# A norm's mean from added channel chunks and one matmul, with new plan costs and ring sizes

## The chip, the cores and the metric

The kernel runs on one core of a Trainium2 chip. The core has five engines that matter here: TensorE (matrix products, called PE in the profile), VectorE (DVE), ScalarE (ACT), GpSimd (POOL) and SyncE (SP), which issues nearly all DMAs. The metric is the device time of one execution in microseconds (us); lower is better. The time before is 3247.18 us, the median of three runs (3243.28 to 3256.7).

## What is computed

The input `x` has 8 images of 384 channels and 1024 pixels, in fp32. Everything below is per pixel (token) unless it says otherwise. The reference, cut to what matters:

```python
def _ln_c(v, eps=1e-6):                       # the norm over channels
    m = jnp.mean(v, axis=1, keepdims=True)
    s = jnp.var(v, axis=1, keepdims=True)
    return (v - m) / jnp.sqrt(s + eps)
...
# conv part: a selective state-space layer and an MLP
t = (t - mu) * rsqrt(var + 1e-05) * ln_w + ln_b
xm, z = split(t @ in_proj_w.T)                # 384 -> 2 x 768
xc = silu(causal_conv3(xm) + conv_b)
dt, Bm, Cm = split(xc @ x_proj_w.T)           # 24, 16, 16
dt = softplus(dt @ dt_proj_w.T + dt_proj_b)
h = exp(dt * A) * h + dt * xc * Bm            # scan over the 1024 tokens, 768 x 16 states
y = (sum_n(h * Cm) + xc * D) * silu(z)
t = gelu(y @ out_proj_w.T @ mlp_w1.T + b) @ mlp_w2.T + b
x = x + t
# ffn part: only images 0 to 4 get one, images 5 to 7 leave it out (zero rows of the quantiser)
t = x;  t = t + quant(gelu(quant(norm(t) @ sign(W1).T + b1)) @ sign(W2).T + b2)
```

Each image is a group of its own for the absolute maximum by which `quant` scales.

## The kernel before

Channels lie on the 128 partitions, in `KC` = 3 chunks of 128; the 1024 tokens are worked in two halves of `T` = 512. For image (batch) b there are four pieces of work:

- `s1` (L648): the norm, the input projection (`p_in`, `p_z`), the convolution, `p_dbc`, `p_dt`, and the products `dtx` = `xc` times `dt`. Results go to DRAM tensors.
- `s2`/`scan` (L812, L825): the scan, in 12 steps `m` per batch. A step loads `dtx_r` and two `dt_r` tiles, each broadcast over partitions by the DMA; for each of four quads of states POOL multiplies by B (L941, `product`), ACT takes two exponentials into PSUM tiles `da` (L550), DVE runs two scans (L966), POOL or DVE multiplies by C, and TensorE sums into `py` (L906). Batches 0 and 7 run by halves with a carried state, the other six over all 1024 tokens.
- `s3` (L1000): output projection (`p_out`) and MLP (`p_h`, `p_o`).
- `ffn` (L1204): norm, two binarised products (`p_y`), two quantisations; batches 0 to 4.

Nothing of the order is written by hand. Every piece of work is an `Op` with an engine and a cost in us, and `Plan.run` (L246) walks through time on these costs, picks the next op of an engine by rank, and emits the instructions in that order. An op can name another engine in `others`, and goes there as a guest when that engine could start it at least `HOST` = 0.3 us before its own engine is free, and be done before the work of its own. Ranks: the scan first, then `s1` up to the next batch (at first up to batch 4), then `s3` and `ffn`; DVE and POOL take ready work that isn't scan work first (L281 to L284). When TensorE would stand idle longer than 0.7 us, filler matmuls (`spare`, L444) are put in. On the chip each engine then runs its list in order and waits on semaphores.

Tiles come from rings: a ring of n buffers lets n tiles of that name live at once. Those that the change touches: `front` (7; pairs of `xc`, `z` and `dt` in s1), `w_f` (3; s1's weights), `dt_r` (3; two used in each scan step), `sq` (1; the square in a norm, the `dtx` tiles before their store, the diagonal in `quant_scale`). `mm` (3) is the PSUM ring of matmul outputs.

The norm (L583) runs 26 times: 16 in s1, 10 in ffn. Its mean before: `columns` (L586) sums over channels with 12 column-tiled matmuls of 32 output rows each, four abreast, so the sums of 512 tokens lie as four strips of 128; ACT (or DVE) scales them by -1/C; `spread` (L601) brings them to all partitions with four matmuls against slices of the identity, and DVE adds the result to the three chunks (L622). The variance then goes the same way by `Square`, `columns`, a turn, a power on POOL, and `spread` with `turned=True`.

Plan costs that the change touches: `MM` (a 128x512 fp32 matmul), `SWITCH` (added per `py` batch), `LAG` (how much before its end an engine counts as free), `c_pair` (POOL's product), and the landing time of a DMA in `Plan.add` (L205).

Of the kernel before, what the change touches and what calls it, by code (L numbers as in the profile page):

```python
# [27 lines left out]
AF = mybir.ActivationFunctionType  # L28
# [42 lines left out]

MM = 0.86
SWITCH = 0.22
# [13 lines left out]
LOAD_TABLE = 1.29  # L87
LAG = {"ACT": 0.09, "DVE": 0.08}

# [9 lines left out]
def c_pair(n):  # L99
    return 0.22 + n * 0.00188  # L100

# [78 lines left out]
class Op:  # L180
    __slots__ = (
        "engine", "cost", "emit", "prio", "slack", "table", "size",
        "wants", "next", "ready", "tiles", "others", "settle", "land",
    )


class Plan:
# [12 lines left out]
    def add(self, engine, cost, emit, r=(), w=(), claim=(), table=None, size=0, others=None,  # L200
            land=1.6, rate=350e3):
        op = Op()
        op.engine, op.cost, op.emit, op.table = engine, cost, emit, table
        op.others, op.settle = others or {}, None
        op.size, op.land, op.prio = 0.03 + size / rate, land + 0.2, (*self.prio, len(self.ops))  # L205
        op.next, op.ready, op.tiles = [], 0.0, []
        op.slack = SLACK if self.prio[0] < 0 else 0.0
# [38 lines left out]
    def run(self):  # L246
# [5 lines left out]
        free["PE"] = 2 * SIGNAL  # L252
        table, dma_free, clock = None, 0.0, Clock()
        left, scanned = len(self.ops), 0
# [17 lines left out]
        def choose(e, now, able):  # L272
            able = [op for s, op in able if s <= now]
            if e == "ACT":
                same = [op for op in able if op.table == table and table != "exp"]
                plain = [op for op in able if op.table in (None, "exp")]
                able = same if table is not None and same else plain or able
                if len(self.spare.ring.free) <= SCARCE:
                    able = [op for op in able if self.spare.ring in map(ring_of, op.tiles) and (
                        op.table in (None, "exp", table))] or able  # L280
            if e in ("DVE", "POOL"):  # L281

                able = [op for op in able if op.prio[0] > 0 and op.ready <= now - PATIENCE] or [
                    op for op in able if op.prio[0] == 0] or able  # L284
            return min(able, key=rank)
# [27 lines left out]
        while left:  # L313
# [28 lines left out]
            if e == "PE":  # L342
                while now - free[e] > IDLE and self.spare.ring.free[0:] and (
                    self.spare.ring.free[0] + SIGNAL <= free[e]
                ):

                    ring = self.spare.ring
                    heapq.heappop(ring.free)
                    self.spare.real = ring.make(self.spare.shape, self.spare.name)
                    self.fill()  # L350
                    free[e] = clock.run(free[e], MM / 2)
                    heapq.heappush(ring.free, free[e])
            for t in taken_by(op):
                heapq.heappop(t.ring.free)
                t.ring.taken[t.lane] += 1
                t.real = t.ring.make(t.shape, t.name)
            op.emit()
            cost = op.cost
            if op.table is not None and op.table != table:
                cost += LOAD_TABLE  # L360
                table = op.table
            end = clock.run(now, cost) if e == "PE" else now + cost
            free[e] = end - LAG.get(e, 0.0)
            if e == "SP":
# [19 lines left out]
class Layer:  # L384
    def __init__(self, ctx, tc, a, out):
# [9 lines left out]
        def ring(tag, bufs, where=sbuf):  # L395
# [6 lines left out]

            "front": ring("front", 7), "t_f": ring("t_f", 2), "w_f": ring("w_f", 3),
            "dbc": ring("dbc", 1), "halo": ring("halo", 2),

            "dt_r": ring("dt_r", 3), "dtx_r": ring("dtx_r", 2), "u": ring("u", 3),
            "xr": ring("xr", 1), "zr": ring("zr", 1), "state": ring("state", 1),
# [137 lines left out]

    def act(self, out, in_, func, cost, r, w, table=None, **kw):

# [4 lines left out]
            }),  # L552
            r=r, w=w, table=table,
        )

    def affine(self, out, in_, r, w, bias=0.0, scale=1.0, n=T, pool=False):
# [21 lines left out]
        else:  # L578
            others = {"DVE": (c_dve(n) + (0 if isinstance(scale, float) else 0.15), on(nc.vector))}
        extra = 0.0 if plain else 0.09 if isinstance(scale, float) else 0.18  # L580
        self.plan.add("ACT", 0.16 + n * 0.00083 + extra, on_act, r=r, w=w, others=others)

    def norm(self, t, eps, scale):  # L583

        nc, add = self.nc, self.plan.add
        def columns(src, name):  # L586
# [35 lines left out]
        add("DVE", c_dve(KC * T), lambda: nc.vector.tensor_add(  # L622
            t.real, t.real, p_mean.real.unsqueeze(1).to_broadcast([P, KC, T])
        ), r=[p_mean], w=[t])
# [6 lines left out]
        p_turned = self.piece("mm", [P, G], "p_turned")  # L631
        add("PE", 0.3, lambda: nc.tensor.matmul(
            p_turned.real, var.real, self.ident[:, ::DQ], start=True, stop=True
        ), r=[var], w=[p_turned])
        rstd = self.piece("root", [P, G], "rstd")
        add("DVE", 0.1, lambda: nc.vector.tensor_scalar_add(rstd.real, p_turned.real, eps),
            r=[p_turned], w=[rstd])
# [10 lines left out]
    def s1(self, b):  # L648
# [45 lines left out]
        for half, cols in enumerate(HALVES):  # L694
# [58 lines left out]

            add("PE", 0.15 + KC * MM, low, r=[w, *all_m], w=[p_dbc], claim=[dbc])
            self.affine(lambda dbc=dbc: dbc.real, lambda p_dbc=p_dbc: p_dbc.real, [p_dbc], [dbc])
# [12 lines left out]
            for k in range(0, KD, 2):  # L768
# [14 lines left out]

                add("PE", MM + 0.2, two, r=[dbc, *dict.fromkeys(ws)], w=pds, claim=[dt.pieces[k // PER]])
                for i in range(2):
# [39 lines left out]
    def scan(self, b, half, state):  # L825
# [21 lines left out]
        for m in range(KC * per_p):  # L847
# [12 lines left out]
            def unit(name, p=p):  # L860
# [7 lines left out]
            xr = unit("xc")  # L868
            self.act(lambda py=py: py.real, lambda xr=xr: xr.real, AF.Identity, c_act(T),
                     r=[xr], w=[py], scale=skip[:, m : m + 1])  # L870
# [18 lines left out]
            for q in range(NQUAD):  # L889
# [43 lines left out]
    def scan_pair(self, u, cols, n, dts, dtxs, bq, cq, state, half, on_pool):  # L933
# [153 lines left out]
    def binarise(self, name, kt, n_out):  # L1087
# [25 lines left out]
        for ks, ms in pieces:  # L1113
# [11 lines left out]

            add("PE", 0.25 + MM, total, r=[w], w=[pm])
            if ks.stop == kt:
# [10 lines left out]
        p_mean = self.piece("mm", [P, NUM_GROUPS, 2], "p_means")  # L1138
        add("PE", 0.3, lambda: nc.tensor.matmul(
            p_mean.real, self.ones[:rows, :], sums.real[:rows], start=True, stop=True  # L1140
# [29 lines left out]
    def quant_scale(self, mx, n):  # L1170
# [11 lines left out]

        add("PE", 0.25, lambda: nc.tensor.matmul(
            p_max.real, self.ones, diag.real, start=True, stop=True
# [196 lines left out]
```

## Time and profile before

| what | value |
|---|---|
| median of 3 runs | 3247.18 us (3243.28 to 3256.7) |
| the profiled execution | 3251.59 us, span 3249.5 us |
| mean granted TensorE clock | 0.982 |
| PE busy | 3136.0 us |
| DVE busy | 2607.3 us |
| ACT busy | 2025.7 us |
| POOL busy | 2749.4 us |
| DMA | 751.89 MB, mean 231 GB/s |

The page lists busy time of each engine, the span in 40 slices of 81 us (a digit is tenths of busy time), the chain of work that ended last, groups of instructions by line, and the DMA issues. A group's row reads: line, engine, operation, output<-inputs, shapes, count | busy us, mean ns of one | idle before it and what ended that. A wait's row reads: who waited <- for whom: us in total, times, the longest. Matmul records are pipelined and an fp32 matmul shows as two records.

### The profile page before, as it was taken

What the parts mean: (1) busy time and instruction counts of PE and PEld (TensorE: products, weight loads), DVE (VectorE), ACT (ScalarE), POOL (GpSimd) and SP (SyncE); (2) the same over time, 40 slices, a digit from 0 to 9 for tenths busy, and PEclk for the clock granted to TensorE, in tenths of its full rate; (3) what the DMA queues carried; (4) which work ended last, traced back from release to release, by engine and by line L of the source; (5) the groups of instructions that cost most, each with busy time, mean ns of one, the idle gap of its engine ahead of it and who ended that gap; (6) DMA issues with size and microseconds to landing.
All of it is one profiled execution on the core that took longest, in us unless ns stands there. A gap on an engine that the chain in (4) does not pass through costs nothing.

```text
span 3249.5 us, 34179 instructions
## 1 busy us (share of the span) xinstructions
PE 3136.0 (97%) x11088; PEld 1308.8 (40%) x11088; DVE 2607.3 (80%) x2078; ACT 2025.7 (62%) x2406; POOL 2749.4 (85%) x1051
## 2 busy tenths in 40 slices
PE   9889899999999998999999999899999999999999
PEld 4333333334443344443443443343344454333334
DVE  3687788988979878887799798698798988787870
ACT  4777677785585656557655755466656465555651
POOL 1777888988889998998988999889999999889870
PEclk9899999999999999999999999999999999999999
DMA  6799778785785667858767666786776666656542
GB/s 214 257 319 302 230 247 284 273 282 192 251 308 190 200 208 268 284 199 273 233 238 283 209 202 209 271 276 223 247 253 235 220 210 212 220 175 195 158 126 79
DMA packets 348977, 751.89 MB, mean 231 GB/s; under 512 B 36480, under 2 KB 113792, under 8 KB 339584
## 3 DMA queue, kind: packets, MB, share of 16 engines
q1 hardware_dynamic: 348368, 749.61, 69.1%
q8 instruction: 89, 1.46, 0.2%
q14 instruction: 88, 0.72, 0.1%
q10 hardware_dynamic: 432, 0.09, 0.0%
HBM read 569.21 MB, written 180.36 MB: 231 GB/s over the span
## 4 chain that ended last, share of the span: by engine, by line
PE 69%; DVE 9%; ACT 7%; DMA 6%; POOL 5%; issue 3%; SPq 1%; DVEq 0%; POOLq 0%; ACTq 0%
PE p_y L534 18%; PE p_h L534 11%; PE p_o L534 11%; PE py L906 8%; PE p_z L534 6%; PE p_out L534 5%; PE p_in L534 5%; POOL u L941 4%; DVE u L966 4%; DVE da L966 2%; ACT da L550 2%; ACT L550 2%; PE p_dt L779 1%; PE spare L444 1%; DMA w_f<-in_in_proj_w 1%
## 5 line engine op out<-in xcount | busy, mean ns | idle before, releaser
L941 POOL TENSOR_TENSOR u<-dtx_r,bc 128x2048 f32<-128x2048 f32 (+1 forms) x360 | 1186.1, 3310 | 133.5 <-PE py L906 82.1
L550 ACT ACTIVATE da<-dt_r,a_neg 128x1024 f32<-128x1024 f32 (+1 forms) x960 | 898.9, 945 | 540.3 <-DVE u L966 306.8
L941 POOL TENSOR_TENSOR u<-u,bc 128x2048 f32<-128x2048 f32 (+1 forms) x274 | 901.2, 3292 | 148.0 <-DVE u L966 133.2
L966 DVE TENSOR_TENSOR_SCAN u<-da,u 128x1024 f32<-128x1024 f32 (+1 forms) x436 | 870.1, 2007 | 153.1 <-ACT da L550 75.3
L534 PE MATMUL p_h<-t,w_b 128*128 128x512 f32 x1152 | 515.5, 599 | 11.1 <-DMA w_b<-in_mlp_w 5.7
L534 PE MATMUL p_o<-g,w 128*128 128x512 f32 x1152 | 514.0, 600 | 9.9 <-DMA w<-in_mlp_w 5.3
L966 DVE TENSOR_TENSOR_SCAN da<-da,dtx_r 128x1024 f32<-128x1024 f32 (+1 forms) x192 | 382.7, 2016 | 91.1 <-POOL dtx_r L941 67.4
L941 POOL TENSOR_TENSOR dtx_r<-dtx_r,bc 128x2048 f32<-128x2048 f32 (+1 forms) x120 | 397.0, 3314 | 2.0
L534 PEld LDWEIGHTS p_o<-g,w 128*128 128x128 f32 x1152 | 215.7, 191 | 301.3 <-issue 273.4
L534 PEld LDWEIGHTS p_h<-t,w_b 128*128 128x128 f32 x1152 | 214.2, 190 | 298.9 <-issue 255.5
L534 PE MATMUL p_y<-tn,w_b 128*128 128x512 f32 x720 | 326.1, 608 | 3.6 <-DVE tn L642 3.6
L534 PE MATMUL p_y<-gf,w_n 128*128 128x512 f32 x720 | 318.3, 596 | 1.8 <-ACT gf L550 1.7
L906 PE MATMUL py<-u,fold 128*32 128x512 f32 x2304 | 308.6, 633 | 2.4 <-DVE u L988 2.4
L966 DVE TENSOR_TENSOR_SCAN da<-da,u 128x1024 f32<-128x1024 f32 (+1 forms) x140 | 282.8, 2040 | 16.6 <-POOL u L941 8.9
L550 ACT ACT_TABLE_LOAD x217 | 278.4, 1283 | 4.0 <-DMA dt_r<-dt_d 0.2
L534 PE MATMUL p_out<-yg,w 128*128 128x512 f32 x552 | 245.1, 596 | 2.0 <-DMA w<-in_out_proj_w 2.0
L534 PE MATMUL p_z<-t,w_f 128*128 128x512 f32 x504 | 234.4, 613 | 9.2 <-DMA w_f<-in_in_proj_w 3.5
L534 PE MATMUL p_in<-t,w_f 128*128 128x512 f32 x504 | 230.5, 606 | 2.2 <-ACT halo L563 1.0
L534 PEld LDWEIGHTS p_y<-tn,w_b 128*128 128x128 f32 x720 | 136.5, 193 | 189.0 <-issue 168.8
L534 PEld LDWEIGHTS p_y<-gf,w_n 128*128 128x128 f32 x720 | 134.3, 190 | 183.3 <-issue 172.2
L565 ACT ACTIVATE y<-p_y,v_vecs 128x512 f32<-128x512 f32 x144 | 98.5, 684 | 144.3 <-PE p_y L534 120.8
L565 ACT ACTIVATE g<-p_h,v_vecs 128x512 f32<-128x512 f32 x152 | 103.4, 681 | 122.0 <-PE p_h L534 121.6
(132 smaller groups left out, 3306.8 us busy)
## 6 DMA issues: line engine op xcount, KB each, us to landing
dt_r<-dt_d SPq DMA_DIRECT2D x144, 512.0 KB, 5.2
dtx_r<-dtx_d SPq DMA_DIRECT2D x72, 1024.0 KB, 5.8
w_b<-in_mlp_w SPq DMA_DIRECT2D x192, 192.0 KB, 3.4
w<-in_mlp_w SPq DMA_DIRECT2D x96, 384.0 KB, 3.5
w_f<-in_in_proj_w SPq DMA_DIRECT2D x168, 192.0 KB, 4.1
y_d<-y SPq DMA_DIRECT2D x120, 256.0 KB, 4.2
gf<-y_d SPq DMA_DIRECT2D x60, 512.0 KB, 6.9
xc_d<-xc SPq DMA_DIRECT2D x48, 512.0 KB, 6.2
```

The lines of the kernel that those rows point to most:

```text
L444: self.plan.fill = lambda: self.nc.tensor.matmul(self.plan.spare.real[:, : 2 * P], self.ones, self.one.to_broadcast([P, 2 * P]), start=Tru ...
L534: self.nc.tensor.matmul(p.real, w.real[:, w0 + k, :], t.at(k0 + k), start=start and k == 0, stop=stop and k == n - 1,)
L550: lambda: self.nc.scalar.activation(out(), in_(), func, **{k: v() if callable(v) else v for k, v in kw.items()}),
L565: nc.scalar.activation(out(), in_(), AF.Identity, bias=bias, scale=scale)
L779: nc.tensor.matmul(pds[i].real, ws[i].real[rows, (k + i) % KC, :], dbc.real[rows, :], start=True, stop=True,)
L906: nc.tensor.matmul(py.real[g * DQ : (g + 1) * DQ, :], self.fold, hc, start=False, stop=(q == NQUAD - 1), skip_group_check=True,)
L941: nc.gpsimd.tensor_mul(u.real[:, x], t.real[:, x], row.real.unsqueeze(2).to_broadcast([P, n, 2]))
L966: da=da, in_u=in_u: nc.vector.tensor_tensor_scan(to(i), da.real[:, i, :], in_u(i), state.real[:, col : col + 1] if half else 0.0, ALU.mult ...
```

## The change

The mean of a norm is formed in another way. The three chunks of channels are added elementwise into one tile `total` of the `sq` ring, either by POOL in two adds or by DVE in one reduction, as the plan decides; one matmul with a matrix of ones then sums over the partitions and puts the sum on all of them; DVE subtracts it, scaled by -1/C, with one scalar-tensor-tensor instruction. `columns` for the mean, the scaling on ACT and `spread` of the mean go. The way of the variance stays.

In the plan, tiled matmuls (several row or column tiles abreast) are marked. A change between tiled and untiled work costs `MODE` = 0.097 us, and after a tiled op TensorE takes another tiled one if one can start. Several costs change by a few per cent, a lag can be given per op, and a DMA counts as landed 0.3 us sooner than before. Four rings change: `front` 7 to 6, `w_f` 3 to 4, `dt_r` 3 to 2, `sq` 1 to 2. The order of all instructions is planned anew from these.

```diff
-MM = 0.86
+MM = 0.859
+MODE = 0.097
...
-LAG = {"ACT": 0.09, "DVE": 0.08}
+LAG = {"ACT": 0.09, "DVE": 0.08, "POOL": 0.045}
...
 def c_pair(n):
-    return 0.22 + n * 0.00188
+    return 0.19 + n * 0.001905
...
     def add(self, engine, cost, emit, r=(), w=(), claim=(), table=None, size=0, others=None,
-            land=1.6, rate=350e3):
+            land=1.6, rate=350e3, lag=None, tiled=False):
...
-        op.size, op.land, op.prio = 0.03 + size / rate, land + 0.2, (*self.prio, len(self.ops))
+        op.size, op.land, op.prio = 0.03 + size / rate, land - 0.1, (*self.prio, len(self.ops))
...
+        op.lag = LAG.get(engine, 0.0) if lag is None else lag
...
+            if e == "PE" and tiled:
+                able = [op for op in able if op.tiled] or able
...
+            if e == "PE" and op.tiled != tiled:
+                cost, tiled = cost + MODE, op.tiled
             end = clock.run(now, cost) if e == "PE" else now + cost
-            free[e] = end - LAG.get(e, 0.0)
+            free[e] = end - (LAG.get(e, 0.0) if guest else op.lag)
...
-            "front": ring("front", 7), "t_f": ring("t_f", 2), "w_f": ring("w_f", 3),
+            "front": ring("front", 6), "t_f": ring("t_f", 2), "w_f": ring("w_f", 4),
...
-            "dt_r": ring("dt_r", 3), "dtx_r": ring("dtx_r", 2), "u": ring("u", 3),
+            "dt_r": ring("dt_r", 2), "dtx_r": ring("dtx_r", 2), "u": ring("u", 3),
...
-            "mm": ring("mm", 3, psum), "sq": ring("sq", 1),
+            "mm": ring("mm", 3, psum), "sq": ring("sq", 2),
...
-            add("PE", 0.78, emit, r=[src], w=[p])
+            add("PE", 0.79, emit, r=[src], w=[p], tiled=True)
             return p
...
-            add("PE", 0.98, emit, r=[src], w=[p])
+            add("PE", 0.89, emit, r=[src], w=[p])
             return p
 
-        p_sum = columns(t, "p_sum")
-        mean = self.piece("rstd", [P, TG], "mean")
-        self.affine(lambda: mean.real, lambda: p_sum.real, [p_sum], [mean], scale=-1.0 / C, n=TG)
-        p_mean = spread(mean, "p_mean")
-        add("DVE", c_dve(KC * T), lambda: nc.vector.tensor_add(
-            t.real, t.real, p_mean.real.unsqueeze(1).to_broadcast([P, KC, T])
+        total = self.piece("sq", [P, T], "total")
+
+        def in_two():
+            nc.gpsimd.tensor_add(total.real, t.real[:, 0, :], t.real[:, 1, :])
+            nc.gpsimd.tensor_add(total.real, total.real, t.real[:, 2, :])
+
+        def at_once():
+            nc.vector.tensor_reduce(
+                total.real, t.real.rearrange("p k l -> p l k"), AX.X, ALU.add
+            )
+
+        add("POOL", 2.5, in_two, r=[t], w=[total], others={
+            "DVE": (c_dve(KC * T) + 0.02, at_once)
+        })
+        p_mean = self.piece("mm", [P, T], "p_mean")
+        add("PE", MM, lambda: nc.tensor.matmul(
+            p_mean.real, self.ones, total.real, start=True, stop=True
+        ), r=[total], w=[p_mean])
+        add("DVE", c_dve(KC * T) + 0.05, lambda: nc.vector.scalar_tensor_tensor(
+            t.real, p_mean.real.unsqueeze(1).to_broadcast([P, KC, T]), -1.0 / C, t.real,
+            ALU.mult, ALU.add,
         ), r=[p_mean], w=[t])
...
-                    add("PE", SWITCH + BATCH * MM, sums, r=[u for _, u in batch], w=[py])
+                    add("PE", SWITCH + BATCH * MM, sums, r=[u for _, u in batch], w=[py],
+                        tiled=True)
...
-                    0.25 + n * 0.00084, r=[dt_r[i]], w=[da], table="exp",
+                    0.256 + n * 0.00084, r=[dt_r[i]], w=[da], table="exp", lag=0.055,
```

The ops of `p_dbc`, `p_dt` and the column sums in `binarise` are marked `tiled` as well, and some smaller costs (the turn, the small matmuls, the affine on DVE, the skip into `py`) change by up to 0.2 us.

More of the change, by code (lines that the diff above doesn't have):

```diff
@@ L182 @@
         "engine", "cost", "emit", "prio", "slack", "table", "size",
-        "wants", "next", "ready", "tiles", "others", "settle", "land",
+        "wants", "next", "ready", "tiles", "others", "settle", "land", "lag", "tiled",
     )
@@ L204, in add @@
         op.others, op.settle = others or {}, None
-        op.size, op.land, op.prio = 0.03 + size / rate, land + 0.2, (*self.prio, len(self.ops))
-        op.next, op.ready, op.tiles = [], 0.0, []
+        op.size, op.land, op.prio = 0.03 + size / rate, land - 0.1, (*self.prio, len(self.ops))
+        op.next, op.ready, op.tiles, op.tiled = [], 0.0, [], tiled
+        op.lag = LAG.get(engine, 0.0) if lag is None else lag
         op.slack = SLACK if self.prio[0] < 0 else 0.0
@@ L252, in run @@
         free["PE"] = 2 * SIGNAL
-        table, dma_free, clock = None, 0.0, Clock()
+        table, tiled, dma_free, clock = None, False, 0.0, Clock()
         left, scanned = len(self.ops), 0
@@ L352, in run @@
                     heapq.heappush(ring.free, free[e])
+                    tiled = False
             for t in taken_by(op):
@@ L544, in mm3, with act @@
         return p
-    def act(self, out, in_, func, cost, r, w, table=None, **kw):
+    def act(self, out, in_, func, cost, r, w, table=None, lag=None, **kw):
         self.plan.add(
@@ L552, in act @@
             }),
-            r=r, w=w, table=table,
+            r=r, w=w, table=table, lag=lag,
         )
@@ L578, in affine @@
         else:
-            others = {"DVE": (c_dve(n) + (0 if isinstance(scale, float) else 0.15), on(nc.vector))}
+            others = {"DVE": (c_dve(n) + (0.04 if isinstance(scale, float) else 0.15), on(nc.vector))}
         extra = 0.0 if plain else 0.09 if isinstance(scale, float) else 0.18
@@ L631, in norm @@
         p_turned = self.piece("mm", [P, G], "p_turned")
-        add("PE", 0.3, lambda: nc.tensor.matmul(
+        add("PE", 0.14, lambda: nc.tensor.matmul(
             p_turned.real, var.real, self.ident[:, ::DQ], start=True, stop=True
@@ L635, in norm @@
         rstd = self.piece("root", [P, G], "rstd")
-        add("DVE", 0.1, lambda: nc.vector.tensor_scalar_add(rstd.real, p_turned.real, eps),
+        add("DVE", 0.15, lambda: nc.vector.tensor_scalar_add(rstd.real, p_turned.real, eps),
             r=[p_turned], w=[rstd])
@@ L752, in low @@
                         )
-            add("PE", 0.15 + KC * MM, low, r=[w, *all_m], w=[p_dbc], claim=[dbc])
+            add("PE", 0.15 + KC * MM, low, r=[w, *all_m], w=[p_dbc], claim=[dbc], tiled=True)
             self.affine(lambda dbc=dbc: dbc.real, lambda p_dbc=p_dbc: p_dbc.real, [p_dbc], [dbc])
@@ L782, in two @@
                         )
-                add("PE", MM + 0.2, two, r=[dbc, *dict.fromkeys(ws)], w=pds, claim=[dt.pieces[k // PER]])
+                add("PE", MM + 0.2, two, r=[dbc, *dict.fromkeys(ws)], w=pds, claim=[dt.pieces[k // PER]],
+                    tiled=True)
                 for i in range(2):
@@ L868, in scan @@
             xr = unit("xc")
-            self.act(lambda py=py: py.real, lambda xr=xr: xr.real, AF.Identity, c_act(T),
+            self.act(lambda py=py: py.real, lambda xr=xr: xr.real, AF.Identity, 0.25 + T * 0.00084, lag=0.06,
                      r=[xr], w=[py], scale=skip[:, m : m + 1])
@@ L911, in scan @@
                 with self.plan.lane(-1):
-                    add("PE", SWITCH + BATCH * MM, sums, r=[u for _, u in batch], w=[py])
+                    add("PE", SWITCH + BATCH * MM, sums, r=[u for _, u in batch], w=[py],
+                        tiled=True)
                 batch = []
@@ L1124, in total @@
                     )
-            add("PE", 0.25 + MM, total, r=[w], w=[pm])
+            add("PE", 0.25 + MM, total, r=[w], w=[pm], tiled=True)
             if ks.stop == kt:
@@ L1138, in binarise @@
         p_mean = self.piece("mm", [P, NUM_GROUPS, 2], "p_means")
-        add("PE", 0.3, lambda: nc.tensor.matmul(
+        add("PE", 0.22, lambda: nc.tensor.matmul(
             p_mean.real, self.ones[:rows, :], sums.real[:rows], start=True, stop=True
@@ L1181, in quant_scale @@
                  scale=lambda: m1.real)
-        add("PE", 0.25, lambda: nc.tensor.matmul(
+        add("PE", 0.22, lambda: nc.tensor.matmul(
             p_max.real, self.ones, diag.real, start=True, stop=True
```

## The prediction

> **What bounds the kernel now.** I read the page first: the busy shares, the 40 slices, the chain that ended last.
>
> ```profile
> PE 3136.0 (97%) x11088; PEld 1308.8 (40%) x11088; DVE 2607.3 (80%) x2078; ACT 2025.7 (62%) x2406; POOL 2749.4 (85%) x1051
> ...
> PE   9889899999999998999999999899999999999999
> ...
> POOL 1777888988889998998988999889999999889870
> PEclk9899999999999999999999999999999999999999
> ...
> PE 69%; DVE 9%; ACT 7%; DMA 6%; POOL 5%; issue 3%; SPq 1%; DVEq 0%; POOLq 0%; ACTq 0%
> PE p_y L534 18%; PE p_h L534 11%; PE p_o L534 11%; PE py L906 8%; PE p_z L534 6%; PE p_out L534 5%; PE p_in L534 5%; POOL u L941 4%; DVE u L966 4%; DVE da L966 2%; ACT da L550 2%; ACT L550 2%; PE p_dt L779 1%; PE spare L444 1%; DMA w_f<-in_in_proj_w 1%
> ```
>
> TensorE is busy 97% of the span at nearly full clock and carries 69% of the chain; POOL is at 85% and, in slices 10 to 35, at 8 and 9 tenths. The last slice shows POOL and DVE idle: from 3168 us on only the second half of the last batch's output work is left on TensorE, about 80 us that nothing here shortens. So the end is the end of the last scan plus 80 us, and two engines near saturation share the pace before it: TensorE, and POOL with DVE behind it. Who holds POOL up is in its waits (total, times, longest):
>
> ```profile
> POOL u L941 <- DVE u L966: 139.5, 70, 12.1
> POOL u L941 <- PE py L906: 82.1, 35, 5.8
> ...
> POOL dtx L794 <- DMA dtx_d<-dtx: 14.5, 8, 4.6
> ```
>
> Between 400 and 2800 us POOL stands idle for only 202 of 2400 us (its instructions summed over that stretch), and 71 of the 82 us spent waiting for `py` lie before 2700. TensorE, however, runs 172 filler matmuls of L444, half of them after 2500 us: there it has time to spare.
>
> The rows that price the norm, by form (count | busy, mean ns of one | idle before), and one norm's TensorE work in order of time (start, length):
>
> ```profile
> L1228 DVE TENSOR_REDUCE mx<-y 128x1 f32<-128x512 f32 x120 | 79.8, 668 | 11.1 <-ACT y L565 10.8
> ...
> L1278 POOL TENSOR_TENSOR x<-x,y 128x512 f32<-128x512 f32 x30 | 37.8, 1280 | 1.8 <-DMA xc_d<-xc 1.4 <-DMA x<-mid_d 0.2
> ...
> L610 PE MATMUL p_mean<-mean,ident 128*128 128x128 f32 x208 | 29.7, 287 | 5.5 <-ACT mean L565 2.7 <-DVE mean L572 1.9 <-ACT dt L565 0.8
> ...
> L622 DVE TENSOR_TENSOR t<-t,p_mean 128x1536 f32<-128x1536 f32 x16 | 27.9, 1745 | 11.3 <-PE p_mean L610 11.3
> ...
> L758 PE MATMUL p_all<-dbc,join 128*96 128x512 f32 x32 | 17.2, 618 | 3.7 <-DVE xc L714 2.4 <-DVE tn L622 1.0 <-ACT dbc L563 0.4
> ```
>
> ```profile
> 2090.61 0.86 PE L592 MATMUL p_sum<-tn,small 128*32 128x128 f32 x24
> 2091.40 2.84 PE L534 MATMUL p_z<-t,w_f 128*128 128x512 f32 x6
> 2094.08 1.05 PE L610 MATMUL p_mean<-mean,ident 128*128 128x128 f32 x8
> 2094.97 1.06 PE L610 MATMUL p_r<-ident,rstd 128*128 128x128 f32 x8
> ```
>
> The slot is the distance to the next start: 0.79 for the column sums, 0.89 for the spread. Each matmul appears as two records: L610's 208 are 26 norms of four. A 128x512 one keeps TensorE for 0.86, the 16 of `p_all` (L758) too, though its modelled records last longer.
>
> **The change, part by part.** The sum is against the profiled execution, 3251.6 us (span 3249.5), 4.4 above the median of 3247.2.
>
> *TensorE's part of the mean.* Removed per norm: 0.79 + 0.89. Added: one 128x512 with ones, 0.86. That is 0.82 less. The removed sums are also a column-tiled burst; the 149 `py` batches between untiled work take 2.03 where four pieces of streaming take 1.72, so entering and leaving cost 0.31, of which I count 0.2 because 0.79 already holds the exit. 1.02 x 26 norms = 26.5 us. Seven norms start before 390 us, where DMA and latency pace; the other 19 give 19.4. Bounds 0 (filler takes its place) and -26.5. I take **-19.4**, by the chain's 69%.
>
> *The adds.* On POOL: two 128x512 adds of 1.28 (L1278), 2.56 a norm, 66.6 for 26. On DVE: one reduction of 1536 elements read across the chunks; three of L1228's less two overheads is 1.7, and L622's 1.75 is beside it. No row shows the strided read; L794's strided product at 2.38 for 1024 is no dearer than two of L1278's. When a norm's sums start, POOL is inside a 4.09 us product in most of the 19 later cases and has 0 to 3 us idle in the next 6; DVE has 0 to 3. So nothing covers these adds: behind them on POOL stand the scan's products, for which DVE's scans wait. With two thirds on POOL: 12.7 x 2.56 = 32, and 6.3 x 1.75 = 11. The chain passes POOL and DVE only for 14% together although both are over 80% busy; I take a quarter of 43, **+11**; bounds 0 and 66.6. The mean's scaling (0.28, on ACT 19 times, DVE 7) goes: 7.3 us, nothing on the path, for ACT is at 62%; its cover would be gone only if ACT became the bound. The first norm stands alone at 8 us: sum to subtraction is 2.5 there, after it 2.56 + 0.86 plus two signals, **+1.4**. The subtraction as a scalar-tensor form costs 0.06 more (L1055's 0.736 against L922's 0.676): **+1** for 26.
>
> A rule against this choice, beside the rows above: the Trainium skill, "GPSIMD Engine Reference", section 4, gives a two-input elementwise add to VectorE, with GPSIMD about twice as slow. The rows agree (1.28 against 0.68 for 512). Followed everywhere it would make the adds 26 x 1.75 = 45 instead of 66.6. And "TensorEngine Tiling (Array Packing)", section Overview, Theoretical Speedup, promises up to four times for 32-wide outputs: by it the tiled sums cost 0.64 against 0.86 and TensorE would lose 0.22 a norm, +6 in all; the timeline's 0.79, and the 0.89 that the strips then need to be spread, say otherwise.
>
> *Ring of `sq`, 1 to 2.* The square, the three `dtx` tiles of a half and the diagonals share one buffer; each `dtx` waits for the last one's store. POOL's wait for it is 14.5, the chain spends 15.3 in such stores. I take **-12**, bounds -30 and 0.
>
> *`w_f`, 3 to 4.* The chain spends 29.7 us in `w_f` loads, five pieces, four before 440 us. One more buffer can hide part: **-10**, bounds -29.7 and 0.
>
> *`front`, 7 to 6.* Three `xc` and three `z` pieces fill it, so `dt` waits for a `z` store (7.6 to land). The last batch's norms end at 1847 and its scan begins at 2788, so late s1 work is covered; without that lead each of 12 halves could lose 7.6. **+3** for the early batches; at most their four halves, +30.
>
> *`dt_r`, 3 to 2.* Two are in use in each step of the scan. Today one of the next two is loaded some 25 us early. With two, a load starts only after the last exponential on its buffer. From there to the first exponential of the next step the trace has a median of 7.8 us for the first and 7.6 for the second buffer, least 4.1, in the 71 steps of the middle batches. Landing takes:
>
> ```profile
> dt_r<-dt_d SPq DMA_DIRECT2D x144, 512.0 KB, 5.2
> ```
>
> At 5.2 the shortfalls sum to 3 us, at 6 to 14, at 7 to 53, at 8 to 120. SP issues in order and would stand before both loads; the weights and scan rows queue behind it, and TensorE waits for those. **+5**, bounds 3 and 53.
>
> *Plan.* `land` falls by 0.3 us. For `dt_r` the old formula gives 4.9 from issue to landing, the new 4.6; the row says 5.2. TensorE's waits for weights are now 25 us in 18 waits; 18 times 0.3 is **+5**, up to +15. Counting mode changes: the old plan gives a `py` batch 1.94 against 2.03 measured, the new one 2.13, so neither is nearer; but a tiled operation may now follow another. The trace has 270 tiled bursts; 16 joined at 0.31 are **-5**, bounds -20 and 0. `POOL`'s lag and the new product costs match the rows (4.09, 2.14) to 0.01 and cost nothing themselves. What no row prices is the new order of everything. Its nearest measure: the starts of the scans of batches 1 to 6 are 351 to 390 us apart for like work, a scatter of some 15 a batch, so over six independent batches about 37. I take 0 and use this for the range.
>
> Sum: -19.4 + 11 + 1.4 + 1 - 12 - 10 + 3 + 5 + 5 - 5 = -20. 3251.6 - 20 = 3231.6, and less the 4.4 to the median: **3227**.
>
> **Rivals.** *No change:* the end hangs on the scan, and TensorE's gain becomes filler, as after 2500 us already. The first term is 0, the sum -0.6, the time 3247. For it: the filler, POOL's 202 us of idle. Against: the chain's 69%.
>
> *Slower, by POOL:* every later norm's adds go to POOL and push the scan by their full length: 19 x 2.56 = 49 instead of 11, with no gain on TensorE; sum +37, 3284. It decides from about 15 us of unhidden POOL time with the TensorE gain gone (sum about +3), and passes 0.5% at some 29. For it: POOL's slices at 9. Against: POOL also waits 82 us for TensorE.
>
> *Slower, by `dt_r`:* landing grows to 7 us because both loads, `dtx_r` and the rows now meet at each step's start; the 53 in place of 5 makes 3275. For it: `z` stores and `gf` loads already take 7; against: slack of 7.7.
>
> *The change doesn't do what it says:* DVE takes most adds, POOL is untouched; then 19 x 1.75 at a quarter is 8, the time 3224, no different.
>
> **How the numbers follow.** About 0.5%, 16 us, is what a measurement can tell here. Forecast 0.45; no change 0.27; POOL 0.16; `dt_r` or a worse order 0.12. The forecast's own range is 3200 to 3254 (the larger open ends, `sq`, `w_f` and TensorE, taken by halves); the whole reaches from 3180, which is 1.28 times the order's 37 below the forecast, to 3288, just past the POOL case. Chances: faster 0.45, same 0.27, slower 0.28.
>
> **What would show it.** Right: no records of `p_sum`, `p_mean` in 26 pairs of untiled records, TensorE's work down about 26 us with fewer fillers, `dtx` no longer waiting for stores, batch starts earlier from batch 2 on. Wrong: POOL's busy time up by 30 to 66 with the batch starts later; exponentials waiting for `dt_r`'s load (4 us in all now); more waits of TensorE for weights. Scan starts that shift by tens of us with none of these would mean the order decided.

## The result, and the profile after

The changed kernel takes 3206.13 us, median of three runs (3200.2 to 3206.42), against 3247.18: a ratio of 0.9862, 95% interval 0.9824 to 0.99. It is faster by 41 us, 1.4%. The forecast was 3227 in a range of 3180 to 3288. The profiled execution took 3206.13 us, span 3204.3.

The page of the changed kernel: busy time, three rows of the 40 slices, and the chain that ended last.

```profile
PE 3087.3 (96%) x10286; PEld 1265.2 (39%) x10286; DVE 2602.2 (81%) x2058; ACT 2021.0 (63%) x2397; POOL 2803.7 (87%) x1097
...
PE   9898999998999999999999999999999999999999
...
POOL 2878988989989888999988999999989999998890
PEclk9899999999999999999999999999999999999999
...
PE 62%; DVE 12%; DMA 9%; POOL 7%; ACT 6%; issue 3%; SPq 1%; DVEq 0%; POOLq 0%; ACTq 0%
PE p_y L541 15%; PE p_h L541 11%; PE p_o L541 10%; PE py L929 8%; PE p_out L541 6%; POOL u L965 5%; PE p_z L541 5%; PE p_in L541 5%; DVE u L990 4%; DVE da L990 3%; ACT da L557 2%; DMA dtx_r<-dtx_d 2%; ACT L557 2%; DMA dt_r<-dt_d 1%; PE spare L451 1%
```

TensorE is 49 us less busy and carries 62% of the chain instead of 69%; POOL is 54 us busier. The row of the granted clock shows the same tenths as before, but the trace has 84 us at half clock where the one before had 122. In POOL's waits (total, times, longest), the wait for `py` and the wait for `dtx` stores are both shorter:

```profile
POOL u L965 <- DVE u L990: 129.8, 56, 9.1
POOL u L965 <- PE py L929: 49.1, 26, 4.6
...
POOL dtx L817 <- DMA dtx_d<-dtx: 8.5, 3, 5.0
```

The rows that price the norm now, by form (count | busy, mean ns | idle before, releaser):

```profile
L640 PE MATMUL p_mean<-total,small 128*128 128x512 f32 x52 | 28.8, 637 | 1.1 <-POOL total L629 1.1
L643 DVE SCALAR_TENSOR_TENSOR t<-p_mean,t 128x1536 f32<-128x1536 f32 x16 | 28.0, 1749 | 6.4 <-PE p_mean L640 6.4
...
L628 POOL TENSOR_TENSOR total<-t 128x512 f32<-128x512 f32 x14 | 17.9, 1277 | 12.2 <-PE p_mean L640 4.9 <-DMA t<-in_x 4.4 <-issue 1.7
L629 POOL TENSOR_TENSOR total<-total,t 128x512 f32<-128x512 f32 x14 | 17.8, 1272 | 1.1
...
L632 DVE TENSOR_REDUCE total<-t 128x512 f32<-128x1536 f32 x2 | 3.8, 1923 | 1.8 <-DMA t<-in_x 1.8
```

Of 26 sums over chunks the plan put 23 on POOL (14 and 9 pairs of adds of 1.28) and 3 on DVE, where the strided reduction took 1.92. One norm in order of time (start, length); the matmul with ones starts 2.6 us after the adds end, behind other work, and costs TensorE 0.94 to the next start, 0.86 of it streaming:

```profile
1185.43 1.27 POOL L628 TENSOR_TENSOR total<-tn 128x512 f32<-128x512 f32 x1
...
1186.77 1.27 POOL L629 TENSOR_TENSOR total<-total,tn 128x512 f32<-128x512 f32 x1
...
1190.65 1.10 PE L640 MATMUL p_mean<-total,small 128*128 128x512 f32 x2
...
1191.59 2.74 PE L541 MATMUL p_y<-tn,w_b 128*128 128x512 f32 x6
...
1193.28 1.73 DVE L643 SCALAR_TENSOR_TENSOR tn<-p_mean,tn 128x1536 f32<-128x1536 f32 x1
```

**Where the 45 us of span went.** I cut each execution at three places: the first exponential of each batch's scan, the end of the last `yg` product on DVE (the last scan is then done), and the end.

| stretch | before | after | difference |
|---|---|---|---|
| start to first scan | 84.2 | 79.0 | -5.2 |
| scan of batch 0 | 479.3 | 458.9 | -20.4 |
| scans of batches 1 to 6 | 2224.2 | 2238.2 | +14.0 |
| scan of batch 7, to the last `yg` | 377.4 | 359.4 | -18.0 |
| behind the last `yg` | 84.4 | 68.8 | -15.6 |

The middle, where nearly all norms after the start lie and where POOL got its adds, became longer. The gain is at both ends. The last row is the one that the prediction held for fixed ("some 80 us that nothing here shortens"). TensorE's work at the end of the kernel before, in order of time:

```profile
3163.25 1.08 PE L906 MATMUL py<-dtx_r,fold 128*32 128x512 f32 x8
3164.27 3.70 PE L534 MATMUL p_o<-g,w 128*128 128x512 f32 x8
...
3167.80 8.75 PE L534 MATMUL p_out<-yg,w 128*128 128x512 f32 x20
...
3176.39 4.46 PE L534 MATMUL p_out<-yg,w_n 128*128 128x512 f32 x10
...
3183.69 31.06 PE L534 MATMUL p_h<-t,w_b 128*128 128x512 f32 x72
...
3214.59 31.06 PE L534 MATMUL p_o<-g,w 128*128 128x512 f32 x72
```

and of the changed kernel:

```profile
3132.94 1.85 PE L929 MATMUL py<-dtx_r,fold 128*32 128x512 f32 x8
...
3135.60 1.99 PE L541 MATMUL p_out<-yg,w 128*128 128x512 f32 x4 [0.80 <-DVE yg L942]
...
3137.42 1.02 PE L541 MATMUL p_out<-yg,w_n 128*128 128x512 f32 x2
...
3138.72 31.06 PE L541 MATMUL p_h<-t,w_b 128*128 128x512 f32 x72
...
3169.61 31.06 PE L541 MATMUL p_o<-g,w 128*128 128x512 f32 x72
```

The last `yg` product ends at 3165.1 before and at 3135.5 after. What must follow it is six records of `p_out` and 144 of `p_h` and `p_o`, 150 records or 64.4 us. After the change just that follows. Before, another 36 records (15.4 us) of `p_o` and `p_out` stood there, work that could have run earlier and for which TensorE had had no time. So two things set the end: when the last scan is done, and how much of TensorE's other work is still left over then.

The same 45 us can be counted on TensorE, each record taken to the start of the next and a stretch at half clock counted as half lost. `p_sum` and `p_mean` take 24 us less (49.4 to 25.6), the half clock costs 19 less (60.8 to 42.1), filler takes 10 less (89.0 to 79.1), idle time and all other work 4 more each. This is an account and not a cause. In the start and batch 0, which became 25.6 us shorter, the half clock costs 13.6 us less.

### The profile page after: what moved, and what is told of

It reads as the page before. It is cut to its first block, busy times and chain, and to the rows that moved or that the text cites. A ratio compares the mean times of both kernels' runs of the same rounds, so it can differ in the third digit from the quotient of the medians.

```text
span 3204.3 us, 32487 instructions
## 1 busy us (share of the span) xinstructions
PE 3087.3 (96%) x10286; PEld 1265.2 (39%) x10286; DVE 2602.2 (81%) x2058; ACT 2021.0 (63%) x2397; POOL 2803.7 (87%) x1097
## 4 chain that ended last, share of the span: by engine, by line
PE 62%; DVE 12%; DMA 9%; POOL 7%; ACT 6%; issue 3%; SPq 1%; DVEq 0%; POOLq 0%; ACTq 0%
PE p_y L541 15%; PE p_h L541 11%; PE p_o L541 10%; PE py L929 8%; PE p_out L541 6%; POOL u L965 5%; PE p_z L541 5%; PE p_in L541 5%; DVE u L990 4%; DVE da L990 3%; ACT da L557 2%; DMA dtx_r<-dtx_d 2%; ACT L557 2%; DMA dt_r<-dt_d 1%; PE spare L451 1%
```

## The experiments

Every kernel ran beside the kernel before on the same chip (its medians were 3248.3, 3247.0 and 3246.0 in the three groups). Ratios are to it. "Last `yg`" and "left over" are read from the profiled execution as above: left over is the TensorE records behind the last `yg`, without filler and less 150, at 0.429 us each.

| kernel | median us | ratio (95%) | clock | last `yg` | left over |
|---|---|---|---|---|---|
| before | 3247.2 | 1 | 0.984 | 3165.1 | 15.4 |
| changed | 3206.1 | 0.9862 (0.9824 to 0.99) | 0.987 | 3135.5 | 0 |
| f1_mean3 | 3232.0 | 0.9953 (0.9935 to 0.9972) | 0.987 | 3162.7 | 0 |
| f2_pool2 | 3239.7 | 0.9972 (0.9958 to 0.9986) | 0.9845 | 3171.4 | 0 |
| f3_chunk1 | 3249.2 | 1.0002 (0.9984 to 1.0019) | 0.9795 | 3171.9 | 15.4 |
| n1_table | 3243.5 | 0.9982 (0.9965 to 0.9999) | 0.986 | 3159.9 | 15.4 |
| r1_mean | 3239.1 | 0.9973 (0.996 to 0.9987) | 0.984 | 3171.6 | 0 |
| r2_rings | 3230.6 | 0.9954 (0.994 to 0.9969) | 0.990 | 3142.2 | 15.4 |
| r3_costs | 3227.8 | 0.9945 (0.9928 to 0.9962) | 0.986 | 3100.2 | 58.3 |
| r4_oldmean | 3226.8 | 0.9942 (0.9926 to 0.9959) | 0.985 | 3136.0 | 27.5 |
| r5_meancosts | 3233.9 | 0.9968 (0.995 to 0.9985) | 0.9825 | 3134.9 | 27.5 |
| n3_table | 3194.0 | 0.9835 (0.9817 to 0.9852) | 0.987 | 3127.0 | 0 |
| n4_land | 3201.9 | 0.9872 (0.9854 to 0.989) | 0.9875 | 3125.7 | 3.4 |
| n5_mode | 3220.0 | 0.9922 (0.9906 to 0.9938) | 0.983 | 3149.1 | 0 |

The clock is the median over the timed runs of the mean granted TensorE clock; for the kernel before it is that of the runs beside the others, the same in all three groups. It differs between kernels, and no theory below speaks of it. Of the 30 runs of the kernel before in the first group, the four at 0.987 took 3237 us in the median and the four at 0.981 took 3252.5; a straight line through all 30 gives 2.7 us for each 0.001 (2.6 through the 21 of the second group, 1.2 through the 8 of the third). By that slope, an estimate, the clock goes with some 8 of the changed kernel's 41 us and with some 16 of r2_rings' 16, and it costs f3_chunk1 some 12. Whether a new order gains by the clock, or the clock rises because TensorE waits less often, no run here separates.

The theory to test was that TensorE's saved work is what counts. The rivals: the scan with POOL sets the pace, so the adds cost more than TensorE gives; and the order, planned anew, is a draw of luck.

### With the order untouched: what a microsecond of an engine is worth

The first three kernels keep the order of a kernel to the instruction and change only the length of some ops, so no new plan confuses them.

**f1_mean3**, in the changed kernel:

```diff
-        add("PE", MM, lambda: nc.tensor.matmul(
-            p_mean.real, self.ones, total.real, start=True, stop=True
-        ), r=[total], w=[p_mean])
+        def thrice():
+            for _ in range(3):
+                nc.tensor.matmul(p_mean.real, self.ones, total.real, start=True, stop=True)
+
+        add("PE", MM, thrice, r=[total], w=[p_mean])
```

> The changed kernel with its order untouched; the matmul with ones of the mean is issued three times instead of once, so TensorE gets 26 x 2 x 0.86 = 45 us more work and nothing else changes. TensorE theory (TensorE's work sets the end, as the before kernel's output matmuls left over at the end of the last scan say): 3206 + 30 to 45, so 3236 to 3251. Scan theory (POOL and DVE set the pace and TensorE has filler to give): less than 12 more, 3206 to 3218. Order theory (the gain is the luck of a new order): says nothing of this run.

Measured: 3232.0, so 26 us more for 45 us of TensorE, 0.58 each. It falls short of the TensorE theory's lower bound and is far above the scan theory's. Its clock is that of the changed kernel. Nothing is added behind the last `yg` (0 left over); the start, batch 0 and batches 1 to 6 grow by 5.8, 5.9 and 15.6.

**f2_pool2**, in the changed kernel:

```diff
-            nc.gpsimd.tensor_add(total.real, t.real[:, 0, :], t.real[:, 1, :])
-            nc.gpsimd.tensor_add(total.real, total.real, t.real[:, 2, :])
+            for _ in range(2):
+                nc.gpsimd.tensor_add(total.real, t.real[:, 0, :], t.real[:, 1, :])
+                nc.gpsimd.tensor_add(total.real, total.real, t.real[:, 2, :])
```

> The changed kernel with its order untouched; POOL does its two adds of a mean twice, so 23 norms put 23 x 2.56 = 59 us more on POOL. Scan theory: 35 to 59 more, 3241 to 3265. TensorE theory: under 20 more, below 3226. The prediction's weight of a quarter gives 15.

Measured: 3239.7, 34 us more for 59 us of POOL, 0.57 each: between the two theories. A third of it, 11.4, lies before the first scan, where four norms stand in a row and nothing covers them; 17.7 in batches 1 to 6. Its groups by form show who waits:

```profile
L629 POOL TENSOR_TENSOR total<-t 128x512 f32<-128x512 f32 x28 | 35.6, 1273 | 11.6 <-PE p_mean L641 5.1 <-DMA t<-in_x 4.4 <-DMA dtx_d<-dtx 1.1
...
L641 PE MATMUL p_mean<-total,small 128*128 128x512 f32 x52 | 31.5, 691 | 18.3 <-POOL total L630 18.3
```

TensorE's idle time in front of the matmul with ones goes from 1.1 us to 18.3, and POOL ends it. So both engines set the pace at about half their time or more, and neither theory alone holds. Both slopes are rough: the changed kernel's own interval is 12 us to either side, which is 0.2 to 0.3 in each, and f2_pool2's lower clock (0.9845 against 0.987) goes with some 7 of its 34 us.

**f3_chunk1**, in the kernel before:

```diff
-                for k in range(KC):
+                for k in range(1):
...
-                            start=(k == 0), stop=(k == KC - 1),
+                            start=True, stop=True,
```

> The kernel before with its order untouched; the column sums of mean and variance run over the first chunk of channels alone (chunks 1 and 2 are left out of both sums), which takes 8 of 12 tiled matmuls and about 0.43 us from each of 52 bursts, 22 us of TensorE in all, and touches no other engine. TensorE theory: 15 to 22 faster, 3225 to 3232. Scan theory: under 6 faster, 3241 or more.

Measured: 3249.2, ratio 1.0002. Taking about 22 us of TensorE work out of the old order gains nothing, so at first sight the TensorE theory falls for the kernel before. But the clock went down with it; the windows of TensorE show where (us, TensorE busy and records, granted clock, DMA share, GB/s), first of the kernel before, then of this one:

```profile
0.00:80.00 80.00, 72.42 (x376) 0.96 0.64 213
80.00:560.00 480.00, 434.48 (x1635) 0.95 0.82 271
560.00:3130.00 2570.00, 2513.57 (x8789) 0.99 0.69 232
```

```profile
0.00:80.00 80.00, 71.55 (x272) 0.98 0.66 222
80.00:560.00 480.00, 428.43 (x1435) 0.94 0.82 269
560.00:3130.00 2570.00, 2502.58 (x8235) 0.98 0.70 231
```

The timed runs have a median clock of 0.9795 where the kernel before beside them has 0.984: 0.0045 of 3249 is 15 us more lost to the half clock, two thirds of what was taken out. (The two profiled executions have 143 and 122 us at half clock, which is 10 us more lost.) At an equal clock, by the slope above, the kernel would be some 12 us faster, beyond the scan theory's 6 and short of the TensorE theory's 15. So this run decides for neither. What the clock doesn't explain may have sunk into waits: the last norm ends at 2536, and the scans after it leave POOL 17 us idle from 2400 to 2800 and 59 from there to 3168, so what TensorE had saved by then had little to hasten. That is argued from these sums, not shown.

### One part alone, the order planned anew

**r1_mean** is the kernel before with the new mean and nothing else of the change.

```diff
-        p_sum = columns(t, "p_sum")
...
+        total = self.piece("sq", [P, T], "total")
...
```

> The kernel before with the new mean alone: old ring sizes, old plan costs, order planned anew. TensorE theory: the mean is worth 15 to 27 us, so 3220 to 3232. Scan theory: the adds on POOL cost more than TensorE gives, 3247 to 3275. Order theory: anything within 25 of 3247, unrelated to its TensorE work.

Measured: 3239.1, 8 us faster. All of the leftover is gone (15.4 to 0), but the last scan ends 6.5 us later. Its clock is that of the kernel before. Neither theory alone: TensorE's gain arrives at the end, and the later scan takes part of it back.

**r2_rings:**

```diff
-            "front": ring("front", 7), "t_f": ring("t_f", 2), "w_f": ring("w_f", 3),
+            "front": ring("front", 6), "t_f": ring("t_f", 2), "w_f": ring("w_f", 4),
...
-            "dt_r": ring("dt_r", 3), "dtx_r": ring("dtx_r", 2), "u": ring("u", 3),
+            "dt_r": ring("dt_r", 2), "dtx_r": ring("dtx_r", 2), "u": ring("u", 3),
...
-            "mm": ring("mm", 3, psum), "sq": ring("sq", 1),
+            "mm": ring("mm", 3, psum), "sq": ring("sq", 2),
```

> The kernel before with the new ring sizes alone (front 6, w_f 4, dt_r 2, sq 2). The prediction's terms say -12 -10 +3 +5 = -14, so 3233, with the gain before the second batch's scan starts. If the shorter dt_r ring costs, it is above 3250 with exponentials waiting for the load of dt_r. Order theory: within 25 of 3247 either way.

Measured: 3230.6, 16 us faster, where the terms said 14. The first scan starts 6 us earlier and batch 0 takes 10 less, as expected; the last scan's own 10 us less were not foreseen. Leftover stays at 15.4. That the terms came out may be luck: the clock is 0.990 against 0.984, by the slope above some 16 us, as much as the whole gain, and in the profile the half clock costs 17 us less in the start and batch 0. The waits that the terms name moved less: POOL for `dtx` stores 14.5 to 8.1 us, TensorE for weights 25 to 17, and ACT for `dt_r` 4 to 16.

**r3_costs** is the changed kernel with the mean and the ring sizes of before.

```diff
-        total = self.piece("sq", [P, T], "total")
...
+        p_sum = columns(t, "p_sum")
...
-            "dt_r": ring("dt_r", 2), "dtx_r": ring("dtx_r", 2), "u": ring("u", 3),
+            "dt_r": ring("dt_r", 3), "dtx_r": ring("dtx_r", 2), "u": ring("u", 3),
...
```

> The kernel before with the new plan costs alone, the preference for tiled work after tiled work and the earlier landing among them. The prediction's terms say +5 -5, no change, 3247. If the better costs were what gains, 3205 to 3230. Order theory: within 25 of 3247.

Measured: 3227.8, 19 us faster, where no change was forecast. TensorE's end of it, in order of time:

```profile
3098.33 1.08 PE L914 MATMUL py<-dtx_r,fold 128*32 128x512 f32 x8
...
3099.34 15.72 PE L541 MATMUL p_h<-t,w_b 128*128 128x512 f32 x36
...
3114.89 31.06 PE L541 MATMUL p_o<-g,w 128*128 128x512 f32 x72
...
3145.79 8.75 PE L541 MATMUL p_out<-yg,w 128*128 128x512 f32 x20
...
3161.68 31.06 PE L541 MATMUL p_h<-t,w_b 128*128 128x512 f32 x72
...
3192.57 31.06 PE L541 MATMUL p_o<-g,w 128*128 128x512 f32 x72
```

The last `yg` product ends at 3100.2, 65 us earlier than before, and then TensorE works on through 58.3 us that were left over, with one filler matmul between. From there TensorE alone sets the end.

**r4_oldmean** puts the old mean back into the changed kernel.

```diff
-        total = self.piece("sq", [P, T], "total")
...
+        p_sum = columns(t, "p_sum")
...
```

> The changed kernel with the old mean put back: new rings and new plan costs stay. TensorE theory: 15 to 27 slower than 3206, so 3221 to 3233. Scan theory: within 10 of 3206 or faster. Order theory: within 25 of 3206 either way.

Measured: 3226.8, 21 us slower than the changed kernel. The last scan ends at the same time (3136.0 and 3135.5), but 27.5 us of TensorE's work are left over instead of none. This pair speaks most plainly for the TensorE theory: with the scan's end unmoved, the saving came off the tail. It isn't the mean alone, though. Counted as above, `p_sum` and `p_mean` take 21.8 us less in the changed kernel, but the half clock of the two profiled executions costs 21 less too (by the timed clocks, 0.985 and 0.987, some 5 of the 21 us go with it), and filler takes 10 more. And work is left over in whole pieces: r5_meancosts below, with the new mean, has the same 27.5. So the closeness to the prediction's 26.5 is partly chance.

**r5_meancosts** is the changed kernel with the old ring sizes.

```diff
-            "front": ring("front", 6), "t_f": ring("t_f", 2), "w_f": ring("w_f", 4),
+            "front": ring("front", 7), "t_f": ring("t_f", 2), "w_f": ring("w_f", 3),
...
-            "dt_r": ring("dt_r", 2), "dtx_r": ring("dtx_r", 2), "u": ring("u", 3),
+            "dt_r": ring("dt_r", 3), "dtx_r": ring("dtx_r", 2), "u": ring("u", 3),
...
-            "mm": ring("mm", 3, psum), "sq": ring("sq", 2),
+            "mm": ring("mm", 3, psum), "sq": ring("sq", 1),
```

> The changed kernel with the old ring sizes: new mean and new plan costs stay. Theory of two ends (the time is the later of the end of the last scan plus 69 us and the end of TensorE's whole work; the new costs bring the scan forward and leave TensorE the later one): the kernel with new costs alone ended at 3228 with 58 us of TensorE's work left over behind the last scan, and the mean takes 27 us of that away, so 3197 to 3207, with some 30 us still left over and the last scan at 3100 to 3110. If the ring sizes carry their 16 us also here: 3215 to 3225.

Measured: 3233.9; the expectation failed. The leftover did fall, from r3's 58.3 to 27.5, but only because the last scan ends 35 us later: TensorE's own end, the profiled span, went from 3227.7 to 3231.2. What the mean saved (`p_sum` and `p_mean` take 27.0 us instead of 48.6) is made up for by 17 us more filler, 7 more lost to the half clock and 4 more idle. One reading is that the adds hold up the scan, because `total` needs a buffer of the `sq` ring, which in r5 it shares as the only one with the square and the `dtx` tiles. But r4 against r3 shows the last scan 36 us later without any adds, from the new rings alone. The four rings were not tried one by one, so the reason stays open.

### How much is luck of the order

**n1_table** and **n3_table** move one plan constant by 0.001 us, in the kernel before and in the changed one:

```diff
-LOAD_TABLE = 1.29
+LOAD_TABLE = 1.291
```

> The kernel before with one plan constant moved by a thousandth of a microsecond (the ACT table load, 1.29 to 1.291): the same work, the same rings, another order. Order theory: it moves by 15 us or more either way, outside 3232 to 3262. TensorE and scan theories, with the order worth little: within 10 of 3247.

> The changed kernel with one plan constant moved by a thousandth of a microsecond (the ACT table load, 1.29 to 1.291): same work, another order. If the order's luck is small, as the same shift in the kernel before said (-5): 3198 to 3214. Order theory: outside, most likely slower, for the changed kernel would be a lucky draw.

The shift of a thousandth changes the order of the instructions throughout. The kernel before moved by -5 us. The changed one moved by -12, to 3194.0, a little outside its expectation and to the faster side (the two ratios' intervals overlap); nothing says that its own 3206 was a lucky draw. It is the fastest kernel of this study, by luck of order alone. Its clock is the changed kernel's. Two draws are few; they put the order's luck at some 10 us, and differences of that size between the part kernels shouldn't be read.

**n4_land** gives the changed kernel the old landing time:

```diff
-        op.size, op.land, op.prio = 0.03 + size / rate, land - 0.1, (*self.prio, len(self.ops))
+        op.size, op.land, op.prio = 0.03 + size / rate, land + 0.2, (*self.prio, len(self.ops))
```

> The changed kernel with the old landing time in the plan (0.3 us later). The prediction gave the earlier landing a cost of 5 us, so 3201. If the earlier landing is what lets the scan run ahead: 3216 to 3230, with the last scan ending later. Order's luck alone: 3196 to 3216.

Measured: 3201.9, within the order's luck of 3206. So nothing shows that the earlier landing gains or costs.

**n5_mode** takes the preference for tiled work out of the changed kernel:

```diff
-            if e == "PE" and tiled:
-                able = [op for op in able if op.tiled] or able
```

> The changed kernel without the preference for tiled work after tiled work; the cost of a mode change stays in the plan. The prediction gave the preference 5 us, so 3211 with some 265 tiled bursts instead of 237; 28 more at 0.31 us are 9 us of TensorE. If the preference is what gains: 3218 or more. Order's luck alone: 3196 to 3216.

Measured: 3220.0, 14 us slower, with 256 tiled bursts (the trace of the changed kernel has 236). Twenty bursts at 0.31 explain 6 us; the clock, 0.983 against 0.987, goes with some 11; and there is the order's luck. That the preference helps is possible, its size is open. Which of the plan costs gives r3 its 19 us isn't settled: the landing showed no worth in the changed kernel, the preference can be part of it, the corrected costs were not tried alone.

## Why the prediction was right, and where it was wrong

The direction and the range held; the forecast of 0.6% was under half of the 1.4%. That the sum came as near as it did is partly luck: terms too small on both sides, and a plan term of 0 that gave about as much as the whole forecast.

- *"About 80 us that nothing here shortens"* was the step that failed. The tail held 15.4 us of TensorE's work left over, and 15.6 of the gain came from there. The profile before had it: the `p_out` work of 8.7 and 4.5 us behind the last `py` batch is only the first five of six chunks, which don't wait for the last scan.
- *TensorE's part, -19.4 of 26.5.* The price was right: `p_sum` and `p_mean` take 24 us less, before the cost of entering 26 tiled bursts, and filler fell from 172 matmuls to 161. Its worth depends on the rest: -8 alone, +6 on the new costs with old rings, -21 on both.
- *The adds, +11.* Mis-sized. 23 norms on POOL, not two thirds; each us of POOL costs 0.57, not a quarter, so at the slope of f2_pool2 the 59 us are worth 34. POOL's busy time did rise by 54, inside the 30 to 66 that the prediction named as a sign against it, and batches 1 to 6 did become 14 us longer, though every batch still started earlier. POOL's idle time from 400 to 2800 us was 226 and not 202 once overlapping records are counted once. The chain's 5% for POOL said too little of an engine that is at 85%.
- *The first norms, +1.4.* With the mean alone the first scan starts 1.7 later (85.9 in r1_mean against 84.2), as the term said; in the whole change it starts 5.2 earlier. r2_rings, at 78.1, points to the rings, but r4_oldmean, with the same rings, starts at 82.6.
- *Rings, -14 in sum:* -16 measured alone, by a path that the terms don't name as far as the clock carries it. In the changed kernel the wait for `dtx` stores fell from 14.5 to 8.5, half of the term's 12. The shorter `dt_r` ring costs what was foreseen in kind; ACT's waits for its loads, before and after:

```profile
ACT da L550 <- DMA dt_r<-dt_d: 4.1, 3, 2.7
```

```profile
ACT da L557 <- DMA dt_r<-dt_d: 22.3, 20, 3.5
```

22.3 us in 20 waits lie between the 14 and 53 that the slack gave for landings of 6 and 7 us, though the median landing is 5.1; whether late starts or single long landings make them up wasn't read, nor how much of it is on the path.
- *Plan, 0.* Put at nothing, because no row priced a new order: the new costs alone gave -19, with the scan's end 65 us earlier and 43 more us left over on TensorE. The order's scatter, put at 37, was some 10.
- *Against the rivals.* "No change" matches f3_chunk1's time, but that kernel ran at a lower clock, so its mechanism isn't shown. "Slower, by POOL" priced the adds too high (49 against 34 at the measured slope) as the forecast priced them too low, and was outrun by the ends. "The adds go to DVE" did not happen.

The parts sum to what the whole gives: -8, -16 and -19 make -43 against -41. That is partly chance, since costs and rings together gave 20 and not 35, and the mean on top of them 21 and not 8. What the part kernels do show is that on the new costs neither the rings alone (r4, 3226.8) nor the mean alone (r5, 3233.9) gains anything over the costs (r3, 3227.8), and both together give 21 us more. Why they need each other stays open.

## What to carry to other kernels

At the end of a profile, list what the busiest engine still does behind the last op of the other chain, and subtract what must come there: that leftover tells which of the two sets the end, which a busy share of 97% doesn't. But compare TensorE's end as well, since a later scan alone makes the leftover smaller. Price an engine's time with the order untouched, by doing an op twice, before planning anew; doing less need not be worth what doing more costs. And where a planner writes the order, shift one constant by nothing much first, to learn how large a difference its luck can make, and set the granted clocks of the kernels side by side before a small difference is given to the change.

## What the runs showed of the hardware that was not expected

Less work for TensorE came with a lower clock once: f3_chunk1, with some 22 us less to do, had 143 us at half clock against 122 (profiled mean 0.978 against 0.982; timed median 0.9795 against 0.984), mostly in stretches of 3.4 us and multiples of it; the kernel with new rings alone had 63 (timed 0.990). A reduction on DVE that reads across three chunks took 1.92 us for 1536 elements where two rows of unstrided reads said 1.7 to 1.75. The two adds on POOL took 2.63 from the start of the first to the end of the second, 1.4 times that; the Trainium skill's page "GPSIMD Engine Reference", section 4, gives about two for a two-input add, which single instructions on 512 elements show here too (1.28 for an add on POOL against 0.68 for a product on DVE).
